# The first and the last passes of a software-pipelined graph network kernel issued from lists of their own

## The chip, the cores and the metric

The kernel runs on one core of a Trainium2 chip. The metric is the device time of one execution in microseconds (us), the median over several runs. One execution was also recorded by the hardware profiler. Engines are named as the profile names them: PE is the matrix engine, PEld its loading of weights, DVE the vector engine, ACT the engine that evaluates functions, POOL the general engine, SP the engine whose queue starts the DMAs.

## What is computed

Node features x have the shape (128 graphs, 64 nodes, 128), adjacencies adj (128, 64, 64), both float32. An adjacency has random weights between 0.05 and 5 on a symmetric, sparse pattern that includes the diagonal. Four graph layers follow one another, each behind a layer normalisation and a relu, and each is added to its input:

```python
for layer in (L0, L1, L2, L3):
    h = relu(layernorm(x))
    x = x + layer(h, adj)
# L0, continuous filters: every edge weight is expanded into 64 Gaussians, two dense
#   products with a softplus between them give a filter of 128 per edge; a node sums
#   filter * (neighbour's product), then softplus between two products
# L1, hyperbolic attention: nodes go through Moebius products and sums in the Poincare
#   ball; every edge gets a score (product, silu, product, sigmoid); a node sums its
#   neighbours' logarithmic maps by score, then silu between two products, then maps
#   back (tanh, artanh, norms and square roots per node)
# L2: product with D^-1/2 adj D^-1/2, then a dense product and a bias
# L3: messages = (adj^T xs) / degree + xr, then a dense product of [x, messages]
```

## The kernel before

**Tiling.** The 128 graphs are cut into 16 groups of 8. A group's nodes lie in tiles of 128 partitions (two graphs of 64 nodes) by 4 pairs by 128 features. The nodes of every graph are sorted by degree, so that the edges fit a fixed set of slots; layers 0 and 1 then work on slots of edges and not on all 64 by 64. A second version that works on all pairs of nodes stands behind a condition and isn't executed with this input.

**Streams and steps.** Every stage of a group is a Python generator, a stream: `load`, `order` (degrees, sorting, normalised x), `layer0`, `layer1_nodes`, `layer1_edges`, `rest1` (the end of layer 1), `rest2` (layers 2 and 3 and the store). Stages add further streams, such as `normed_x` (layer norm of the sorted x and its first product), `weights_of`, `squares`, `duo`, `filter_of` and `neighbours` in layer 0, `norm_of_h1` in `layer1_nodes`, `coefs_of`, `rows`, `scores_of` and `heads` in `layer1_edges`. The weights are prepared by four streams of their own (`slots_ranks`, `weights0`, `weights1`, `weights2`, group -1), partly through `turned_from`. A stream yields between steps; one step holds a few instructions, nearly always of one engine.

**The order.** Nothing schedules these instructions but their order in the program: the block runs under a manual schedule of PE, DVE, ACT and POOL, so each of the four works through its instructions in the order in which the steps are issued, and waits at the first one whose operand or buffer isn't ready. Only SP's DMAs are placed by the framework. The order is the long string `ORDER`, 492 entries of the form `name@offset`. `run` goes through that string once a pass, for passes -6 to 21. In pass `it` the entry `rest2@-5` issues the next step of `rest2` of group `it - 5`, if there is such a group; `weights0@=1` issues a step of a weight stream in pass 1 only. A pass therefore works on six groups at once, each in another stage. In passes -1 to 4 the later stages have no group yet, and in passes 16 and after the earlier stages have none left: the same string is issued with entries left out. A full pass issues as much as one whole group.

**Function tables.** A step can name a table of ACT ("log" for exp and ln, "silu" for silu and tanh). `step` keeps the last one named in issue order, and puts a table load (L923) in front where it changes, whichever engine the step is for.

**Lines that matter.** In `order`: the sorting product (`graphs_mm`, L1247), L1467 and L1483 (h and its copy with relu in `normed_x`), L1518 (the ranks' product) and L1530 (comparison of slots). In layer 0: the spreading of edge weights L1385, Square L1600 and Exp L1603 in `duo`, the products L1617 and L1634 with Exp L1624 and Ln between them, the multiplication L1639 and the products L1663 in `neighbours`. In layer 1: L2061 and the copies L2059 in `coefs_of`, `scores_of` L2094 to L2103, tanh L2126 in `heads`, L2197 to L2200 (two products and the Silu in `rest1`). In `rest2`: statistics L1267, L1282 (normalisation on ACT, four activations, in `normed_act`), the products of one graph each L1247 and L1254, those of a pair L1240, the scaling L1297, the store L2401. L1801 is a logarithm in `layer1_nodes`, with which a chain of some eighty short steps begins.

The two functions that decide:

```python
def step(self, name, group):
    s = self.streams[name, group]
    _, takes, _, table = s.want
    if table not in (None, self.table):
        self.table = table
        self.scalar.preload_act_table_set({...}[table])
```

Of the kernel before, what the change touches and what calls it, by code (L numbers as in the profile page):

```python
# [774 lines left out]
ORDER = """  # L775
heads20@-4 turned_from5@=2 heads20@-4 duo00@-2 rest2@-5 layer1_nodes@-3 rest2@-5 filter_of00@-2
duo02@-2 rest2@-5 product_with_bias@-3 rest2@-5 slots_ranks@=-2 coefs_of12@-4 weights_of12@-2
coefs_of12@-4 product_with_bias@-3 layer1_nodes@-3 coefs_of12@-4 weights2@=3 neighbours00@-2
rest2@-5 filter_of01@-2 turned_from0@=-4 layer1_nodes@-3 duo02@-2 filter_of00@-2 neighbours00@-2
filter_of00@-2 filter_of01@-2 slots_ranks@=0 weights0@=-2 coefs_of20@-4 layer1_nodes@-3  # L780
coefs_of20@-4 layer1_nodes@-3 layer1_edges@-4 layer1_edges@-4 layer1_nodes@-3 layer1_nodes@-3
weights1@=-5 layer1_edges@-4 layer1_nodes@-3 layer1_nodes@-3 rest1@-4 weights2@=3 layer1_nodes@-3
rest1@-4 layer1_nodes@-3 turned_from1@=-2 rest1@-4 layer1_nodes@-3 neighbours01@-2 filter_of02@-2
rest1@-4 filter_of00@-2 layer1_nodes@-3 neighbours01@-2 filter_of02@-2 filter_of01@-2 squares10@-2
layer1_nodes@-3 rest2@-5 layer1_nodes@-3 layer1_nodes@-3 turned_from2@=0 order@-1 layer1_nodes@-3
layer1_nodes@-3 layer1_nodes@-3 layer1_nodes@-3 layer1_nodes@-3 rest1@-4 layer0@-2 layer1_nodes@-3
order@-1 layer1_nodes@-3 layer1_nodes@-3 rest1@-4 layer1_nodes@-3 layer1_nodes@-3 rest2@-5
layer1_nodes@-3 layer1_nodes@-3 layer1_nodes@-3 layer1_nodes@-3 layer1_nodes@-3 layer1_nodes@-3
filter_of00@-2 layer1_nodes@-3 layer1_nodes@-3 layer1_nodes@-3 layer1_nodes@-3 layer1_nodes@-3
turned_from5@=2 layer1_nodes@-3 filter_of00@-2 layer1_nodes@-3 layer1_nodes@-3 norm_of_sum@-3  # L790
neighbours02@-2 duo20@-2 rest2@-5 weights0@=1 filter_of01@-2 rest2@-5 weights0@=1 filter_of00@-2
filter_of00@-2 filter_of01@-2 norm_of_sum@-3 rest2@-5 filter_of02@-2 neighbours02@-2 duo20@-2
layer1_nodes@-3 duo20@-2 rest2@-5 norm_of_sum@-3 layer1_nodes@-3 layer1_nodes@-3 layer1_nodes@-3
order@-1 filter_of01@-2 rest2@-5 filter_of01@-2 weights2@=2 filter_of03@-2 neighbours03@-2
weights2@=2 rest1@-4 layer1_nodes@-3 weights0@=1 filter_of03@-2 neighbours03@-2 rest1@-4
layer1_nodes@-3 filter_of03@-2 layer1_nodes@-3 squares20@-2 filter_of02@-2 order@-1 norm_of_h@-3
x_self@-4 rest2@-5 filter_of02@-2 weights0@=1 filter_of01@-2 norm_of_h@-3 filter_of02@-2
filter_of02@-2 duo22@-2 weights0@=1 layer1_nodes@-3 filter_of20@-2 duo22@-2 layer1_nodes@-3
duo22@-2 filter_of20@-2 layer1_nodes@-3 layer1_nodes@-3 order@-1 layer1_nodes@-3 filter_of02@-2
neighbours20@-2 filter_of22@-2 attention@-3 neighbours20@-2 layer1_nodes@-3 filter_of20@-2  # L800
weights2@=2 layer1_nodes@-3 order@-1 rest2@-5 layer1_nodes@-3 order@-1 layer1_nodes@-3
layer1_nodes@-3 weights0@=1 rest2@-5 attention@-3 filter_of22@-2 layer1_nodes@-3 filter_of22@-2
filter_of03@-2 turned_from1@=-4 filter_of20@-2 order@-1 duo10@-2 one_minus_z@-3 weights0@=0
one_minus_z@-3 rest2@-5 filter_of03@-2 one_minus_z@-3 layer1_nodes@-3 filter_of03@-2
filter_of03@-2 turned_from0@=-2 one_minus_z@-3 layer1_nodes@-3 order@-1 duo10@-2 one_minus_z@-3
rest2@-5 filter_of03@-2 filter_of20@-2 order@-1 filter_of20@-2 layer1_nodes@-3 layer1_nodes@-3
slots_ranks@=-5 layer1_nodes@-3 layer1_nodes@-3 layer1_nodes@-3 layer1_nodes@-3 layer1_nodes@-3
layer1_nodes@-3 layer1_nodes@-3 layer1_nodes@-3 layer1_nodes@-3 layer1_nodes@-3 order@-1
attention@-3 neighbours22@-2 turned_from3@=-2 order@-1 duo10@-2 rest2@-5 attention@-3
neighbours22@-2 order@-1 duo12@-2 weights2@=2 turned_from4@=1 filter_of10@-2 rest2@-5  # L810
filter_of11@-2 duo12@-2 filter_of10@-2 rest2@-5 filter_of10@-2 order@-1 filter_of11@-2
neighbours10@-2 filter_of22@-2 weights0@=-2 rest2@-5 layer1_nodes@-3 rest2@-5 neighbours10@-2
filter_of10@-2 rest2@-5 order@-1 filter_of22@-2 layer1_nodes@-3 filter_of22@-2 filter_of10@-2
duo12@-2 layer1_nodes@-3 rest2@-5 filter_of11@-2 rest2@-5 filter_of12@-2 neighbours11@-2 order@-1
filter_of11@-2 layer1_nodes@-3 layer1_nodes@-3 turned_from3@=-2 layer1_nodes@-3 weights1@=0
filter_of12@-2 neighbours11@-2 filter_of12@-2 squares12@-2 filter_of10@-2 rest2@-5 weights2@=2
filter_of10@-2 layer1_nodes@-3 filter_of10@-2 layer1_edges@-3 coefs_of02@-3 order@-1
filter_of11@-2 order@-1 rest2@-5 filter_of11@-2 coefs_of00@-3 order@-1 rest1@-4 rest2@-5
filter_of13@-2 neighbours12@-2 neighbours13@-2 filter_of13@-2 neighbours12@-2 filter_of13@-2
neighbours13@-2 filter_of12@-2 rows00@-3 filter_of13@-2 turned_from4@=1 order@-1 rest2@-5  # L820
filter_of11@-2 filter_of12@-2 layer0@-2 rows00@-3 filter_of11@-2 filter_of12@-2 filter_of13@-2
# [49 lines left out]
class Weave:  # L871
# [63 lines left out]
    def run(self, order, groups):  # L935

        steps = [step.rsplit("@", 1) for step in order.split()]
        for it in range(-6, groups + 6):
            for name, off in steps:
                if off[0] == "=":  # L940
                    if int(off[1:]) == it:
                        self.step(name, -1)
# [1511 lines left out]
```

## Time and profile before

| What | Value |
|---|---|
| Time, median of 3 runs | 1788.97 us (1787.3, 1788.97, 1789.33) |
| Time of the profiled execution | 1789.83 us |
| Its span (first to last instruction) | 1788.0 us |
| PE busy | 1580.1 us (88%), 10231 matmuls |
| DVE busy | 1576.3 us (88%), 4872 instructions |
| ACT busy | 1496.0 us (84%), of it 92 table loads of 1283 ns |
| POOL busy | 413.3 us (23%) |
| Mean granted clock of PE | 0.935 of full speed |
| Chain that ended last | PE 48%, ACT 30%, DVE 14% |

All times of instructions, stretches and waits are from the profiled execution, counted from the start of its span. Its time is 1.83 us above its span, and 0.86 above the median. The page gives busy times over the whole span, in 40 slices of 44.7 us, the chain of work that ended last, and the costliest lines; the trace gives a row for each run of equal instructions (start, duration, engine, line, operation, output and inputs, and behind it in brackets how long the engine had been idle and which instruction ended that).

### The profile page before, as it was taken

The page shows a single profiled execution, that of the slowest core. Times are in us where ns is not written, and L with a number is a line of the kernel's source. Part 1 is how long each engine was busy: PE and PEld are TensorE (multiplying, and loading weights), DVE is VectorE, ACT ScalarE, POOL GpSimd, SP SyncE. Part 2 cuts the span into 40 slices and gives each one's busy share as a digit, 9 for nine tenths or more (in the row PEclk, how much of TensorE's full clock was granted, in tenths as well). Part 3 has the DMA queues.
Part 4 walks back from the last instruction along what each step waited for, and adds up shares of the span by engine and source line. Part 5 has one row for each costly group of instructions (what it writes and reads, how often), then busy time and mean ns, then how long its engine had stood idle before and what let it go on. Part 6 is the DMA issues. An engine that isn't in the chain of part 4 may idle for free.

```text
span 1788.0 us, 30233 instructions
## 1 busy us (share of the span) xinstructions
PE 1580.1 (88%) x10231; PEld 855.9 (48%) x10231; DVE 1576.3 (88%) x4872; ACT 1496.0 (84%) x2784; POOL 413.3 (23%) x717
## 2 busy tenths in 40 slices
PE   3969888998989899898989899898989989896853
PEld 2424444545545455454545454554545455454542
DVE  5659799999999999999999999999999999988853
ACT  2858898989899898989899898989989898986632
POOL 1010113123221413223121312322141322302221
PEclk8979999999999999999999999999999999997865
DMA  2000202011110202011020201111020201102110
GB/s 62 6 1 7 57 7 54 11 43 24 27 46 16 58 7 57 17 34 34 16 58 10 60 10 38 30 27 46 16 58 1 50 18 29 36 7 58 33 37 9
DMA packets 57173, 54.22 MB, mean 30 GB/s; under 512 B 13616, under 2 KB 40624, under 8 KB 57008
## 3 DMA queue, kind: packets, MB, share of 16 engines
q1 hardware_dynamic: 57008, 52.19, 11.8%
q8 instruction: 83, 1.36, 0.3%
q14 instruction: 82, 0.67, 0.1%
HBM read 7.61 MB, written 4.19 MB: 7 GB/s over the span
## 4 chain that ended last, share of the span: by engine, by line
PE 48%; ACT 30%; DVE 14%; issue 3%; POOL 2%; DMA 2%; SPq 1%; DVEq 0%; ACTq 0%; POOLq 0%
PE big L1634 7%; PE sm L1240 7%; PE big L2094 6%; PE big L2076 5%; PE big L1617 5%; PE big L1663 4%; ACT ex L1624 4%; PE sm L2120 3%; ACT ex L1627 3%; PE big L2098 3%; ACT e L1600 3%; DVE ex L1639 2%; ACT ra L1669 2%; ACT e L1603 2%; PE sm L1247 2%
## 5 line engine op out<-in xcount | busy, mean ns | idle before, releaser
L1634 PE MATMUL big<-ex,w2T 128*128 128x512 f32 (+1 forms) x768 | 296.5, 519 | 10.4 <-DVE den L1707 5.6
L1639 DVE SCALAR_TENSOR_TENSOR ex<-big,c_L_gnn_b,ra 128x1024 f32<-128x1024 f32 (+1 forms) x160 | 198.4, 1240 | 28.4 <-PE big L1634 27.0
L1617 PE MATMUL big<-e,w1T 64*128 64x512 f32 (+1 forms) x768 | 187.2, 581 | 10.9 <-ACT e L1603 8.3
L1634 PEld LDWEIGHTS big<-ex,w2T 128*128 128x128 f32 x768 | 134.2, 190 | 122.2 <-issue 72.5
L1624 ACT ACTIVATE ex<-big,c_L_gnn_b 128x1024 f32<-128x1024 f32 (+1 forms) x160 | 174.5, 1091 | 7.4 <-PE big L1617 6.9
L2094 PE MATMUL big<-va,U 64*128 64x512 f32 (+1 forms) x768 | 175.3, 532 | 4.9 <-DVE va L2079 4.9
L1663 PE MATMUL big<-va,a 64*128 64x512 f32 (+1 forms) x768 | 176.8, 560 | 2.9 <-ACT va L1584 1.8
L2103 ACT ACTIVATE ex<-big,c_L_gnn_att_b 128x1024 f32<-128x1024 f32 (+1 forms) x160 | 167.6, 1078 | 9.8 <-PE big L2098 9.4
L2098 PE MATMUL big<-slot_r,Sx 64*128 64x512 f32 (+1 forms) x768 | 165.9, 507 | 0.0
L1627 ACT ACTIVATE ex<-ex 128x1024 f32<-128x1024 f32 (+1 forms) x160 | 165.4, 1033 | 0.1
L1669 ACT ACTIVATE ra<-big 128x1024 f32<-128x1024 f32 (+1 forms) x160 | 160.2, 1001 | 3.5 <-PE big L1663 1.7
L1398 DVE TENSOR_TENSOR ex<-ex 128x512 f32<-128x512 f32 (+1 forms) x256 | 140.4, 554 | 1.4
L2214 POOL TENSOR_TENSOR w<-w,hh 128x512 f32<-128x512 f32 x16 | 22.1, 1379 | 454.7 <-DVE w L2206 441.6
L923 ACT ACT_TABLE_LOAD x92 | 118.0, 1283 | 2.2 <-PEq L2442 0.7
L2059 DVE COPY_PREDICATED att<-oh,th 128x256 f32<-128x256 uint16 x256 | 111.4, 446 | 8.2 <-DMA th<-row 8.0
L2076 PE MATMUL big<-oh,pqs 64*64 64x512 bf16 (+1 forms) x1152 | 115.0, 337 | 0.0
L1663 PEld LDWEIGHTS big<-va,a 64*128 64x128 f32 x768 | 73.2, 198 | 87.1 <-issue 47.1
L2079 DVE COPY_PREDICATED va<-slot_r,big 128x1024 f32<-128x1024 uint32 (+1 forms) x96 | 105.2, 1097 | 5.7 <-PE big L2076 5.5
L2120 PE MATMUL sm<-ex,aw2b 128*32 128x512 f32 (+1 forms) x640 | 98.0, 593 | 11.0 <-ACT ex L2103 11.0
L2098 PEld LDWEIGHTS big<-slot_r,Sx 64*128 64x128 f32 x768 | 73.6, 187 | 59.9 <-issue 59.9
L1254 PE MATMUL big<-adjT,v 64*128 64x64 f32 x256 | 31.5, 424 | 74.5 <-ACT v L1282 74.5
L1617 PEld LDWEIGHTS big<-e,w1T 64*128 64x128 f32 x768 | 65.4, 197 | 63.9 <-issue 28.6
(570 smaller groups left out, 3678.0 us busy)
## 6 DMA issues: line engine op xcount, KB each, us to landing
th<-row SPq DMA_DIRECT2D x128, 256.0 KB, 3.5
th<-row SPq DMA_DIRECT2D x64, 104.0 KB, 2.2
x<-in_x_dram SPq DMA_DIRECT2D x16, 256.0 KB, 2.8
out_dram<-v SPq DMA_DIRECT2D x16, 256.0 KB, 2.3
adj<-in_adj_dram SPq DMA_DIRECT2D x16, 128.0 KB, 2.4
e<-in_L_gnn_att_w_dram SPq DMA_DIRECT2D x2, 64.0 KB, 4.4
bR<-in_L_gnn_mlp_w_dram SPq DMA_DIRECT2D x2, 64.0 KB, 3.6
wupd<-in_L_gnn_W_upd_dram SPq DMA_DIRECT2D x1, 128.0 KB, 3.4
```

Of the source, the lines that this page charges most:

```text
L1617: T.matmul(dst, lhsT=w1T[HALF[h], :], rhs=e[HALF[h], b, 0:W], start=True, stop=True)
L1624: act(ex[:, :, 0:wide], pre[:, :, 0:wide], AF.Exp, bias=b1)
L1627: act(ex[:, :, 0:wide], ex[:, :, 0:wide], AF.Ln, bias=1.0)
L1634: T.matmul(wf[:, b, cols], lhsT=w2T, rhs=ex[:, b if c < 2 else b ^ j, cols], start=True, stop=True)
L1639: V.scalar_tensor_tensor(two.rearrange("q (j r) -> q j r", j=2), wf[:, :, 0:wide], b2s, ra[:, :, 0:wide], ALU.add, ALU.mult)
L1663: T.matmul(nb[:, b, at * W:at * W + W], lhsT=rf[rows, p + j, :], rhs=factors[0][rows, k + j, :], start=True, stop=True)
L1669: act(ra[:, :, 0:wide], nb[:, :, 0:wide], AF.Copy)
L2076: T.matmul(rk[h, k, 0:W], lhsT=pqs[h, s, p, :], rhs=oh[h, p, at:at + W], start=s == 0, stop=s == 2)
L2094: T.matmul(pre[:, b, col], lhsT=U[h, p + k, :], rhs=coefs[h, k, :], start=True, stop=False)
L2098: T.matmul(pre[:, b, col], lhsT=Sx[s][h, p + k, :], rhs=slot_r[h, at:at + W], start=False, stop=s == 1)
L2103: act(a[:, :, 0:wide], pre[:, :, 0:wide], AF.Silu, bias=ab1)
L2120: T.matmul(sl[here, 0:wide], lhsT=aw2b, rhs=a[:, b, 0:wide], start=True, stop=True)
```

## The change

The string `ORDER` loses its entries for one pass only and is used for passes 6 to 13 alone. All that the passes before it issued now stands in a list `HEAD`, and all that the passes behind it issued in a list `TAIL`. The lists are written out: each entry gives a stream by its number in `NAMES` and a group (in `HEAD` as it is, in `TAIL` counted from 16), and is one step. `HEAD` has 1476 steps and `TAIL` 2159 of the 7228 in all. They hold the same steps as before, in another order.

```diff
 ORDER = """
-heads20@-4 turned_from5@=2 heads20@-4 duo00@-2 rest2@-5 layer1_nodes@-3 rest2@-5 filter_of00@-2
...
+heads20@-4 heads20@-4 duo00@-2 rest2@-5 layer1_nodes@-3 rest2@-5 filter_of00@-2 duo02@-2 rest2@-5
...
 """
+CYCLES = range(6, 14)
+NAMES = """
+heads20 turned_from5 duo00 rest2 layer1_nodes filter_of00 duo02 product_with_bias slots_ranks
...
+"""
+HEAD = """
+8@-1 8@-1 8@-1 18@-1 18@-1 18@-1 43@-1 43@-1 20@-1 24@-1 24@-1 20@-1 15@-1 15@-1 15@-1 79@0 15@-1
...
+"""
+TAIL = """
...
+3@-1 3@-1
+"""
...
-    def run(self, order, groups):
-
-        steps = [step.rsplit("@", 1) for step in order.split()]
-        for it in range(-6, groups + 6):
+    def run(self, groups):
+
+        names = NAMES.split()
+        steps = [step.rsplit("@", 1) for step in ORDER.split()]
+
+        def listed(order, base):
+            for step in order.split():
+                k, g = step.split("@")
+                self.step(names[int(k)], base + int(g))
+
+        listed(HEAD, 0)
+        for it in CYCLES:
             for name, off in steps:
-                if off[0] == "=":
-                    if int(off[1:]) == it:
-                        self.step(name, -1)
-                elif 0 <= it + int(off) < groups:
-                    self.step(name, it + int(off))
+                self.step(name, it + int(off))
+        listed(TAIL, groups)
...
-        w.run(ORDER, GROUPS)
+        w.run(GROUPS)
```

Two short stretches show how the lists differ, written as stream@group#step:engine. The first steps of `normed_x` of group 0, before and after:

```text
before  order@0#16 to #18:DVE  turned_from4  order@0#19:DVE  normed_x@0#0:DVE
        sums_of_columns@0#0:POOL  normed_x@0#1 to #3:POOL  normed_x@0#4:PE  normed_x@0#5:ACT
after   order@0#13:ACT  sums_of_columns@0#0:POOL  normed_x@0#0:DVE  normed_x@0#1 to #3:POOL
        normed_x@0#4:PE  normed_x@0#5:ACT  order@0#14:DVE  order@0#15:PE  order@0#16 to #18:DVE
```

And in pass 18, where only the last groups are left:

```text
before  rest1@14#8:PE  ...  scores_of00@15#0:PE  scores_of01@15#0:PE  ...
        scores_of00@15#1:ACT  scores_of01@15#1:ACT
after   rest1@14#8:PE  ...  scores_of00@15#0:PE  scores_of00@15#1:ACT
        scores_of01@15#0:PE  scores_of01@15#1:ACT
```

## The prediction

> **What bounds the kernel now.** I read the slices of the page first. The kernel is full in the middle and thin at both ends:
>
> ```profile
> PE   3969888998989899898989899898989989896853
> ...
> DVE  5659799999999999999999999999999999988853
> ...
> PEclk8979999999999999999999999999999999997865
> ```
>
> One slice is 44.7 us. The first four slices and the last four are the only ones with low digits. Then I took the busy times by stretch. Passes were found by counting each engine's instructions in the order of the list: pass 6 begins at 411 us, pass 14 at 1230. Each full pass takes 102.3 us: the stores of groups 0 and 11 begin at 371.2 and 1496.7, and (1496.7 - 371.2) / 11 = 102.3. Columns are the stretch, its length, then busy us of PE, PEld, DVE, ACT, POOL, then the granted clock.
>
> ```profile
> 0.00:45.00 45.00, 17.77 (x98) 10.66 (x100) 26.14 (x88) 13.39 (x21) 8.78 (x34) 0.85 0.26 62
> 45.00:70.00 25.00, 24.86 (x155) 12.52 (x153) 14.36 (x28) 22.32 (x28) 0.19 (x1) 0.93 0.04 11
> 70.00:125.00 55.00, 38.46 (x151) 18.31 (x146) 30.60 (x79) 31.38 (x58) 6.27 (x7) 0.78 0.00 1
> ...
> 411.00:1230.00 819.00, 770.41 (x5108) 416.37 (x5104) 776.28 (x2401) 747.33 (x1396) 206.61 (x347) 0.97 0.13 32
> 1230.00:1536.00 306.00, 287.80 (x1910) 155.86 (x1914) 291.54 (x902) 279.35 (x519) 76.04 (x128) 0.97 0.12 30
> ...
> 1635.00:1707.00 72.00, 51.70 (x355) 31.56 (x355) 58.65 (x224) 40.71 (x97) 18.31 (x35) 0.77 0.16 40
> 1707.00:1740.00 33.00, 20.09 (x115) 15.37 (x115) 14.80 (x46) 9.81 (x27) 8.19 (x10) 0.63 0.09 21
> ```
>
> In the middle DVE is busy 776 of 819 us and PE 770: both bound, and that part is untouched. Outside it PE is busy about 344 us in the first 411 and 465 in the last 558; at the middle's 94% these would take 366 and 494 us. So about 45 us at the front and 64 at the back are lost to chains with nothing beside them. That is the ceiling for any new order, not the forecast.
>
> **What the change moves.** The two lists hold exactly the steps that the first six and last seven passes issued, with the same places where they begin and end, so all arithmetic and the 818 us between stay. The queue of DMA issues on SP keeps its order. No group is started a pass earlier: the work of the same engine that stands ahead of a step differs by 0.4 to 1.6 us on average in every pass. So only waits between neighbours can change. The program has 86 table loads where it had 92; the six that go are three silu/log pairs of the last passes. I walked the places where an engine sits idle, with the durations of the trace.
>
> **A, fill, -1.9 us.** The rows that matter, from the timeline (start, duration, engine, line):
>
> ```profile
> 31.65 1.08 POOL L1467 TENSOR_TENSOR a<-xp,o_mv 128x512 f32<-128x512 f32 x1
> ...
> 34.29 3.50 DVE L1385 TENSOR_TENSOR va<-oh,adjT 128x1024 f32<-128x1024 bf16 x3
> ...
> 36.75 1.14 ACT L1483 ACTIVATE a<-sm,sr 128x128 f32<-128x128 f32 x4 [2.22 <-PE sm L1240]
> ...
> 40.80 1.28 ACT L923 ACT_TABLE_LOAD   x1
> ...
> 42.10 1.06 ACT L1603 ACTIVATE e<-e 128x1024 f32<-128x1024 f32 x1
> ```
>
> HEAD puts normed_x of group 0 directly behind the copy of xp (ACT, ends 23.0) instead of behind the slot comparisons (L1530); weights1's last DVE step also goes ahead. Its DVE part (1.2) then ends at 24.2, not 30.2; POOL's h comes 2.5 us later at 26.7, the transposes (1.1) end at 27.9. But L1518 now stands behind them on PE: it ends at 28.2 instead of 25.9, and the DVE work after it (0.42 + 2.36 + 0.27 + 3.00) ends at 34.3, where it ended before. So the spread L1385 gains nothing; the stall moved from PE to DVE. What gains is ACT: L1483 is done at 32 instead of 37.9, so squares00 runs at 35.5, squares02 behind its operand at 36.7, the first Square of duo at 37.8, the load at 38.9, the Exp at 40.2, against 42.10. That is 1.9. From 45 to 70 PE is busy 24.86 of 25 us, so all that follows moves along and nothing is added. Bounds: 3.6 gained (the PE wait before L1617 at 43.2), 1.0 lost if DVE waits longer for L1518.
>
> **C, first nodes chain, -1.3.** Between 106 and 120 us ACT waits four times for the chain of layer1_nodes. The Exp of group 1's first duo (L1603, 1.04 us) runs at 120.47, behind that chain; HEAD issues it at about 112.5, in a gap. ACT is busy 24.8 of the 25 us from 125, so the microsecond counts; 0.3 more comes from the DVE step L1304, no longer behind a weights2 step. Bounds 0 and -1.8.
>
> **B and D, 45-92 and 125-411: 0.** PE or ACT is full and the work is the same. Bounds +3 and -3: small reorderings in passes 3 to 5.
>
> **E, passes 14 to 17, -2.** Each pair of loads removed looks like this:
>
> ```profile
> 1286.67 2.57 ACT L923 ACT_TABLE_LOAD   x2
> ...
> 1289.26 1.11 ACT L1624 ACTIVATE ex<-big,c_L_gnn_b 128x1024 f32<-128x1024 f32 x1
> ```
>
> Six loads of 1.28 us are 7.7 us of ACT. ACT is busy 279 of 306 us there, DVE 292 and PE 288: not ACT's time but DVE's sets the pass, so I take a quarter of it. To save the pair, the list puts rest1's product (L2197) 7 us of PE work later in two of the three cases; its Silu (L2200) stands where it stood on ACT. Bounds: -7.7 if ACT's time is all on the path, +8 by the second rival.
>
> The Trainium skill, "ScalarE: Activation LUTs", "What ACT_TABLE_LOAD costs", gives 1283 ns for a load and 1380 ns more for a drain, 2.66 us in all; by it E's ceiling would be 16 us as an estimate. The rows agree on the first and show no second: L1624 begins 20 ns after the loads.
>
> **F, last group's nodes, -1.7.** On ACT at 1630 us, and on the same chain five microseconds later:
>
> ```profile
> 1635.07 0.59 ACT L2126 ACTIVATE row<-sm,hab 128x416 f32<-128x416 f32 x1
> ...
> 1636.20 1.65 ACT L1282 ACTIVATE v<-x,k_s,k_r 128x128 f32<-128x128 f32 x4 [0.54 <-DVE k_s L2309]
> ...
> 1637.87 1.28 ACT L923 ACT_TABLE_LOAD   x1
> ...
> 1639.16 0.21 ACT L1801 ACTIVATE nn<-nn 128x8 f32<-128x8 f32 x1
> ```
>
> TAIL moves norm_of_h1 (1.28 us of ACT) into the 1.10 us wait before L2272 at 1629.8, which brings the heads at 1635.07 to about 1634.3 (-0.8). It then puts the load and L1801 ahead of rest2's L1282. The logs follow at 1636.1 instead of 1639.2, but L1282 still stands before the next ACT step of the chain (at_p, 1640.2), which ends up at 1638.5. Of the 1.7, 0.8 is the first move and 0.9 the second. DVE is dense for the ten microseconds after it, then the chain runs alone to 1672, so I let the 1.7 through. Bounds 0 and -2.9. What is late next is PE: from 1672.7 to 1701.8 it has no gap, so TAIL's other moves there (rows00 earlier, last copies) are worth 0.
>
> **G, last two groups side by side, -2.1.**
>
> ```profile
> 1710.92 1.66 DVE L2061 SCALAR_TENSOR_TENSOR th<-th,oh 128x832 f32<-128x832 f32 x1 [1.91 <-DMA th<-row]
> 1715.74 1.12 DVE L1297 SCALAR_TENSOR_TENSOR v<-sm,dn,x 128x128 f32<-128x128 f32 x4
> ```
>
> L1297 (rest2 of group 14) is ready at 1713.0, when PE's L1240 ends, and waits behind seven DVE instructions of group 15. TAIL puts it directly behind L2061: 1713.1. The permutation steps follow (0.42, PE 0.37, DVE 0.45 + 0.48), L1247 starts at 1715.7 instead of 1719.2. The steps of group 15 that it overtook then take DVE until 1718.9, so the statistics L1267 start there, not at 1721.8, and L1282 at 1721.7 instead of 1724.7. On PE the transposes stand behind rest1's L1254, which ends at 1723.1, and end at 1724.7 against 1726.8: 2.1 remain, and carry through L1240 and L2383 to rest1's L2197 (1732.5 before). After L2197 the chain of group 15 is alone and its order is the same: 0 to the end. Bounds 0 and -3.5.
>
> **The sum:** -1.9 - 1.3 + 0 - 2 - 1.7 - 2.1 = -9.0 us. It is made on the profiled execution, 1789.83 us with a span of 1788.0, which is 0.86 above the median. Taken off the median of 1788.97: 1780.0.
>
> The Trainium skill, "TensorE: Matmul & The Clock Gate", Part 1, says that a window of about 3.4 us without PE work halves its clock. This trace agrees in kind: the clock is 0.63 in 1707-1740, and eight matmuls of L1240 take 2.08 us at 1710.9 but 1.16 at 1735.5. By the rule denser ends would also run faster, perhaps 3 us more as an estimate; the sum has none of it.
>
> **Rivals.** *Hidden anyway:* each walk assumes that the chain it shortens is the one that sets the end. If only G survives, the gain is 2.1 us: 1787. For it speaks A, where one moved wait came straight back. What a measurement can tell from no change is about 0.2%, 3.6 us. Chance 0.15.
>
> *Tighter passes (slower):* passes 4, 5 and 14 to 17 ran at the middle's 102.3 us, and the lists re-interleave them too. In the one list a consumer stands behind enough other work; some now stand closer. In pass 14 the DVE mask L1515 of order stands seven steps further up, about 1.7 us of DVE work sooner against the ACT copy it reads; DVE is in order, so all behind it waits, and DVE has only 4.8 us of slack a pass (14.5 idle in three). One or two such waits a pass, 2.5 us, in six passes are +15; with E gone and A, C, F, G kept (-7.0) that is +8: 1797. It decides above 1.8 us a pass. Against it: I found only two to five such places a pass, none above 2.6 us. Chance 0.21.
>
> *Looser passes:* the same re-interleaving takes a third of DVE's 4.8 idle us from six passes, -10 more: 1770. Chance 0.20.
>
> That the change does nothing is excluded by the order of the two programs: some steps move on every engine but SP.
>
> **The numbers.** The forecast, -3.6 to about -14, has 0.44; with the looser passes faster is 0.64, same 0.15, slower 0.21. All bounds at once would reach 1767 and 1801; they will not meet. The range is 1768 to 1796: about 0.07 below it, 0.13 above. The likeliest case alone is 1775 to 1785.
>
> **What would show it.** Right: Exp L1603 first at about 40 us; stores of rest2 still 102.3 apart in the middle; L2197 of the last group still about 50 us before the last store is issued (1732.5 and 1782.5 now), with L1247 of group 14 some 4.8 us behind the start of L2061 instead of 8.3; 86 loads. Wrong: the first L1603 not earlier; the stretch from pass 14 to the store of group 12 longer than before; new DVE waits on ACT copies (L1515) or on PE (L1639) in passes 4, 5, 14 to 17.

## The result and the profile after

| Kernel | Median, us | Runs, us |
|---|---|---|
| before | 1788.39 | six, 1787.3 to 1789.33 |
| after | 1797.28 | six, 1795.17 to 1798.64 |

The ratio is 1.0048, with an interval of 1.0037 to 1.0058: slower by 8.9 us, where 1780.0 was forecast. The profiled execution took 1797.08 us, its span 1795.3. Lines of the kernel after have numbers 217 higher (L1603 is L1820, L1639 is L1856); the experiments' kernels have shifts of their own.

From the page of the kernel after, the busy times, the slices and the chain that ended last:

```profile
PE 1585.7 (88%) x10231; PEld 848.8 (47%) x10231; DVE 1596.2 (89%) x4872; ACT 1493.9 (83%) x2778; POOL 419.8 (23%) x717
...
PE   5879898998989899998989899898989989897863
...
DVE  5759799999999999999999999999999999998863
...
PE 40%; ACT 29%; DVE 22%; issue 3%; POOL 2%; DMA 2%; SPq 1%; DVEq 0%; ACTq 0%
```

The first two slices and those at the end are fuller, as the prediction wanted. But DVE is busy 19.9 us longer than before (1576.3) with the same 4872 instructions, and its share of the chain went from 14% to 22%.

I took the end of every step in both traces and compared them pass by pass. A minus says that the kernel after was ahead: -6.4 us at 117 to 122 us, -5.2 in pass 2, -2.1 in pass 4, +2.0 in pass 6, +0.4 in passes 10 to 13, +6.4 in pass 15, +11.6 in pass 17, +6.4 in pass 19, +7.2 at the end. So the fill gained more than forecast and lost it all by pass 6; passes 14 to 17 lost 11; the end gave back 5.

The windows of three passes of the old tail, one line a pass (stretch, length, then busy us of PE, PEld, DVE, ACT and POOL, the clock, the DMA share, GB/s), before:

```profile
1245.00:1347.00 102.00, 96.15 (x639) 51.97 (x638) 97.09 (x302) 93.29 (x175) 25.63 (x43) 0.97 0.13 32
1347.00:1449.20 102.20, 96.43 (x639) 52.20 (x638) 97.07 (x302) 93.37 (x175) 25.57 (x43) 0.97 0.12 30
1449.20:1551.40 102.20, 96.44 (x639) 52.34 (x638) 96.51 (x298) 93.25 (x175) 25.56 (x43) 0.97 0.11 28
```

and between the same steps after:

```profile
1244.80:1353.40 108.60, 99.93 (x647) 52.28 (x646) 102.13 (x311) 94.56 (x175) 27.56 (x43) 0.97 0.12 30
1353.40:1458.50 105.10, 95.60 (x642) 50.27 (x645) 100.26 (x299) 94.11 (x175) 27.97 (x43) 0.98 0.12 29
1458.50:1562.70 104.20, 97.04 (x637) 51.02 (x637) 99.43 (x298) 90.04 (x172) 26.46 (x43) 0.97 0.11 28
```

The passes are 11.5 us longer, DVE is busy 11.1 us longer in them, and its idle time hardly changes (15.7 and 16.1 us). PE and ACT have nearly the same work (by the counts in the rows PE 9 matmuls more, ACT 3 instructions fewer) and more idle time. Whatever happened, happened inside what the page calls DVE's busy time.

**Theory 1, pairs.** The timeline of DVE shows how. Three steps of `rest1` of group 11 (L2261, L1327, L1329) with what stands between them, before:

```profile
1414.22 0.16 DVE L2261 TENSOR_SCALAR d_s<-d_hn 128x4 f32<-128x4 f32 x1
1414.29 0.44 DVE L2059 COPY_PREDICATED att<-oh,th 128x256 f32<-128x256 uint16 x1
1414.63 0.16 DVE L1327 TENSOR_SCALAR ah<-d_s 128x4 f32<-128x4 f32 x1
1414.70 0.42 DVE L1740 TENSOR_SCALAR a<-a 128x512 f32<-128x512 f32 x1
1415.03 0.17 DVE L1329 RECIPROCAL ah<-ah 128x4 f32<-128x4 f32 x1
```

and the same steps after:

```profile
1421.94 0.16 DVE L2478 TENSOR_SCALAR d_s<-d_hn 128x4 f32<-128x4 f32 x1
1422.01 0.42 DVE L1957 TENSOR_SCALAR a<-a 128x512 f32<-128x512 f32 x1
1422.34 0.16 DVE L1544 TENSOR_SCALAR ah<-d_s 128x4 f32<-128x4 f32 x1
1422.54 0.18 DVE L1546 RECIPROCAL ah<-ah 128x4 f32<-128x4 f32 x1
```

An instruction's record is its entry in the trace, from its start to its end. An instruction whose operand is older begins some 80 ns before its predecessor's record ends: L1957 at 1422.01, L2478 ends at 1422.10. L1546 reads what L1544, directly ahead of it, wrote. It begins 40 ns after that record's end. Over the whole trace of before the first kind has a median of -83 ns, the second of +34 ns: 117 ns a pair, two neighbours of which the second needs the first. A step that overwrites what the one ahead has read or written begins as late, and counts too. In the old string steps of other streams stand between such neighbours, and TAIL and HEAD put many side by side. By the programs there are 785 such pairs before and 975 after, 66 more in HEAD and 124 more in TAIL. The lost overlap counts as busy time, which is why DVE looks busier with the same work.

The rivals that the experiments had to exclude: the waits on PE and ACT that the prediction's slower rival named (theory 2), the table loads, and the changed order as such, whatever its pairs (theory 3). The clock is none: the mean granted clock is 0.941 in the profiled execution, and was 0.935 before.

The account of DVE's time between two marks (the same step of `layer1_nodes` in two groups) is read from the traces. The columns add up to the length: the records' durations; the gaps inside pairs, with the pairs' number; the other gaps up to 60 ns, nearly all overlaps; and the waits over 60 ns.

| Stretch | Kernel | Length, us | Records | Pairs | Other gaps | Waits |
|---|---|---|---|---|---|---|
| three passes, HEAD | before | 296.5 | 326.5 | +5.1 (129) | -53.1 | 18.0 |
| | after | 304.9 | 326.0 | +7.8 (188) | -47.7 | 18.7 |
| three passes, TAIL | before | 306.4 | 354.1 | +5.4 (130) | -63.1 | 10.1 |
| | after | 317.9 | 358.0 | +8.3 (213) | -55.9 | 7.5 |

In HEAD's stretch 59 more pairs cost 2.7 in their own gaps and 5.4 in overlap that is gone, 8.1 of 8.4 us. The waits are a net sum there. DVE waits 2.82 us for PE at 124 us, where it did not wait before, and the other waits of the stretch got shorter by 2.1. That wait alone takes the lead at the start of the stretch from 6.4 to 3.6 us; e1 has it too, with 1.69 us, and e3, which leaves HEAD's order at 117 us, has none. So for HEAD no run separates the wait's share from that of the pairs. In TAIL's stretch 83 more cost 2.9 and 7.2, 10.1 of 11.5; the waits are 2.6 less, and the records 3.9 more, of which seven instructions that now fall between the marks are 2.3, and steps held by POOL (last section) 2.2, less small differences.

### The profile page after: what moved, and what is told of

Its sections match the earlier page's. It is cut to its first block, busy times and chain, and to the rows that moved or that the text cites. A ratio compares the mean times of both kernels' runs of the same rounds, so it can differ in the third digit from the quotient of the medians.

```text
span 1795.3 us, 30197 instructions
## 1 busy us (share of the span) xinstructions
PE 1585.7 (88%) x10231; PEld 848.8 (47%) x10231; DVE 1596.2 (89%) x4872; ACT 1493.9 (83%) x2778; POOL 419.8 (23%) x717
## 4 chain that ended last, share of the span: by engine, by line
PE 40%; ACT 29%; DVE 22%; issue 3%; POOL 2%; DMA 2%; SPq 1%; DVEq 0%; ACTq 0%
PE big L1851 7%; PE sm L1457 6%; PE big L2311 5%; PE big L2293 4%; PE big L1834 4%; DVE ex L1856 3%; PE big L1880 3%; ACT ex L1841 3%; PE sm L2337 3%; ACT ex L1844 2%; ACT e L1817 2%; PE big L2315 2%; ACT ra L1886 2%; ACT ex L2320 2%; DVE ex L1615 2%
## 5 line engine op out<-in xcount | busy, mean ns | idle before, releaser
L1851 PE MATMUL big<-ex,w2T 128*128 128x512 f32 (+1 forms) x768 | 301.8, 524 | 7.6 <-DVE den L1924 3.8
L1856 DVE SCALAR_TENSOR_TENSOR ex<-big,c_L_gnn_b,ra 128x1024 f32<-128x1024 f32 (+1 forms) x160 | 198.0, 1238 | 26.6 <-PE big L1851 24.1
L2320 ACT ACTIVATE ex<-big,c_L_gnn_att_b 128x1024 f32<-128x1024 f32 (+1 forms) x160 | 167.8, 1078 | 21.1 <-PE big L2315 20.7
```

Of the source, the lines that this page charges most:

```text
L1851: T.matmul(wf[:, b, cols], lhsT=w2T, rhs=ex[:, b if c < 2 else b ^ j, cols], start=True, stop=True)
L1856: V.scalar_tensor_tensor(two.rearrange("q (j r) -> q j r", j=2), wf[:, :, 0:wide], b2s, ra[:, :, 0:wide], ALU.add, ALU.mult)
L2320: act(a[:, :, 0:wide], pre[:, :, 0:wide], AF.Silu, bias=ab1)
```

## The experiments

Ratios are to the kernel before, run on the same chip, with 95% intervals.

| Kernel | Pairs | Median, us | Before, us | Ratio |
|---|---|---|---|---|
| e1_head | 851 | 1790.68 | 1789.23 | 1.0010 (1.0000 to 1.0019) |
| e2_tail | 909 | 1796.29 | 1789.23 | 1.0038 (1.0023 to 1.0054) |
| e3_ends | 803 | 1781.05 | 1789.23 | 0.9957 (0.9944 to 0.9971) |
| e4_apart | 835 | 1805.69 | 1789.23 | 1.0094 (1.0079 to 1.0110) |
| e5_adjacent | 937 | 1810.89 | 1789.07 | 1.0115 (1.0099 to 1.0132) |
| e6_loads | 785 | 1789.44 | 1789.07 | 0.9999 (0.9990 to 1.0008) |
| e7_last_first | 800 | 1777.82 | 1789.07 | 0.9933 (0.9919 to 0.9946) |
| e8_tail_adjacent | 913 | 1809.24 | 1790.29 | 1.0108 (1.0093 to 1.0124) |
| e9_from_pass17 | 805 | 1776.96 | 1790.29 | 0.9925 (0.9912 to 0.9939) |
| e10_last_first_again | 800 | 1777.31 | 1790.29 | 0.9930 (0.9917 to 0.9944) |
| e11_fill_pairs | 481 | 1789.02 | 1788.92 | 0.9999 (0.9990 to 1.0008) |
| e12_fill_else | 785 | 1793.94 | 1788.92 | 1.0030 (1.0019 to 1.0040) |
| e13_free_before | 729 | 1786.51 | 1788.64 | 0.9983 (0.9974 to 0.9992) |
| e14_free_adjacent | 809 | 1793.39 | 1788.64 | 1.0027 (1.0016 to 1.0039) |
| e15_free_after | 883 | 1795.02 | 1788.64 | 1.0029 (1.0017 to 1.0041) |

e13 has 56 pairs fewer than before, not the 53 of its expectation.

### One list at a time: e1_head, e2_tail

In the kernel after, the other list's steps are put back in the order of the old string (the lists shortened to a description here):

```diff
 HEAD = ...                      # e1_head keeps it
-TAIL = ...
+TAIL = """the same steps in the order of the old string"""
# e2_tail: the same with HEAD
```

> HEAD as in the changed kernel, and behind pass 13 the one list as before. Theory 1 (pairs): a DVE step that stands directly behind the DVE step whose result it reads starts 34 ns after that one's end in both traces, any other 83 ns before its predecessor's end, so each such pair costs 117 ns of DVE; the program of before has 785 pairs, this one 851, and 66 x 0.117 = 7.7 us are lost in passes 3 to 5, against the 6.4 us that the fill gains up to 122 us. Theory 2 (waits): the loss in passes 3 to 5 is stalls behind other engines, such as 2.8 us of DVE before the filter's multiplication at 124 us. Both expect the shift that the changed kernel shows in its middle: +0.4 us against before, within 1 us. If the two lists act on one another, it is off by more than 2 us.

> The one list as before up to pass 13, and TAIL behind it. From the shift of the changed kernel's steps: +11 us in passes 14 to 17, -4.5 in the last two passes, in all +6.7 us against before. Theory 1 explains the +11 by 24 + 33 + 26 + 29 = 112 more pairs in these four passes, 112 x 0.117 = 13.1 us, less what the idle time of DVE takes; theory 2 by waits for PE and ACT, of which the trace of the changed kernel shows no more on DVE in passes 14 to 17 than before (about 14 against 18 us). Time: +5 to +8 us by both.

With HEAD alone the steps are ahead by 5.0 us in pass 2, behind by 2.7 in pass 6, and 1.5 behind from there to the end. With TAIL alone the steps stay within 1.5 us of before up to pass 13, then they are at +1.5, +4.9, +8.2, +9.6 in passes 14 to 17, and +6.4 at the end. The two add up to the change (1.5 and 7.1 us by the medians, 8.9 in all). Each list gains at its outer end and loses where it re-interleaves passes that were already full.

### The ends only: e3_ends

HEAD is kept for its first 275 steps, up to 117 us, and TAIL for its last 396 (passes 18 to 20); all between goes back to the old order (described, not printed, here too).

```diff
-HEAD = <1476 steps of the new list>
+HEAD = <first 275 of the new list, the rest in the old order>
-TAIL = <2159 steps of the new list>
+TAIL = <old order, then the last 396 of the new list>
```

> HEAD's order only up to step 20 of layer1_nodes of group 0 (117 us), then the one list's order for what is left of passes 1 to 5; the one list for 6 to 17; then TAIL's order for the steps that passes 18 to 20 issued. 803 pairs against 785 and 975. If passes 3 to 5 and 14 to 17 are where the lists lose and nothing else, both ends keep their gain: -6.4 at the front, -4.5 at the end, +2 for 18 pairs: -9 us, between -11 and -6. If a lead at the front is taken back by the full passes whatever their order (the changed kernel's shift went from +2.0 in pass 6 to +0.4 in pass 9, so a pass has some play), only the end is left: -5 to -3.

1781.05: 8.2 us faster than before, and 16 faster than after. The lead of 7.3 us that the fill makes now survives through all passes to pass 17, and the last passes add 3 (the profiled execution, 1779.39, is the fastest of the five). So the gains forecast for the two ends are there, and they carry. What ate them was the middle of each list.

### Pulling the pairs apart again: e4_apart

Both new lists, with a rule that takes a DVE step of another stream from up to five places further on where a stream's next DVE step would follow directly:

```diff
+def other(self, todo):
+    dve = [key in self.streams and self.streams[key].want[0] == DVE for key in todo[:6]]
+    if dve[0] and todo[0] == self.last:
+        for j in range(1, len(dve)):
+            if (dve[j] and todo[j] not in todo[:j] and self.ready(self.streams[todo[j]])):
+                return j
+    return 0
...
-            for step in order.split():
-                k, g = step.split("@")
-                self.step(names[int(k)], base + int(g))
...
+            while todo:
+                self.step(*todo.pop(self.other(todo)))
```

> Both lists of the changed kernel, with one rule in their issue: where the next step is a DVE step of the stream that issued the last DVE step, the next ready DVE step of another stream among the five entries behind it is issued first. 835 pairs against the changed kernel's 975; PE, ACT and POOL keep their order, and the table loads stay at 86. Theory 1: 140 pairs x 0.117 = 16.4 us less of DVE, three quarters of it on the path: -12 us against the changed kernel, -8 to -16, so -3 against before. Theory 2: the held back steps only come later, and nothing that DVE waits for is earlier: 0 to +4 against the changed kernel, +9 to +13 against before.

It has 140 pairs fewer than the kernel after and is 8.4 us slower: theory 1's number was missed, with the wrong sign, and theory 2's 0 to +4 as well. The account of TAIL's three passes shows what the rule gives and takes there:

| Kernel | Length, us | Records | Pairs | Other gaps | Waits |
|---|---|---|---|---|---|
| after | 317.9 | 358.0 | +8.3 (213) | -55.9 | 7.5 |
| e4_apart | 317.9 | 356.5 | +5.9 (152) | -59.5 | 15.1 |

61 pairs fewer give back 2.4 and 3.6, 6.0 us, as the theory has it. The waits grow by 7.6, so this stretch is as long as in the kernel after. The loss comes elsewhere: HEAD's stretch is 2.3 us longer, with some 5 us more of waits, and the middle keeps e4 3.6 us behind the kernel after; of the 5 us that the last passes gave the kernel after, e4 gets 2. In the answer on DVE's waits in that stretch (us in total, times, longest), three of after:

```profile
DVE e L2236 <- ACT pqs L2234: 2.1, 2, 1.5
...
DVE ex L1856 <- PE big L1851: 0.4, 2, 0.2
DVE rt L2207 <- ACT e L2195: 0.3, 1, 0.3
```

and the same of e4_apart:

```profile
DVE e L2244 <- ACT pqs L2242: 3.1, 2, 2.1
DVE ex L1864 <- PE big L1859: 2.2, 4, 0.9
...
DVE rt L2215 <- ACT e L2203: 1.4, 1, 1.4
```

A step pulled ahead had its place in the list, but not yet its operand, as far as these rows tell; they are 3.9 of the 7.6 us. Parting a pair with a step that isn't ready did not pay here.

### More pairs, nothing else moved far: e5_adjacent, e8_tail_adjacent

The opposite experiment on the kernel before. If the stream that ran last on DVE has its next DVE step one or two places further on, that step is issued first. In e5 this holds in passes 6 to 13, for `rest1` and `rest2`; in e8 in passes 14 to 17, for `filter_of` too.

```diff
+def same(self, todo):
+    for j in range(1, min(3, len(todo))):
+        if (todo[j] == self.last and self.last[0] in ("rest1","rest2") and todo[j] in self.streams
+                    and self.streams[todo[j]].want[0] == DVE and self.ready(self.streams[todo[j]])
+                    and todo[j] not in todo[:j]):
+            return j
+    return 0
```

> The program of before with one rule in passes 6 to 13 alone, where the changed kernel has the same list as before: a DVE step of rest1 or rest2 whose stream issued the last DVE step is moved up by one or two entries, directly behind it. 937 pairs against 785, 19 more in each of the eight passes; PE, ACT and POOL keep their order, and every moved step comes earlier, the step it passes later by 0.1 to 0.2 us. Theory 1 (a pair costs 117 ns of DVE): 152 x 0.117 = +17.8 us, or less by what the 5 us of idle DVE in a pass take up: +10 to +18. Theory 2 (only waits for other engines cost): nothing that waits for PE, ACT or POOL moves by more than 0.2 us: 0, within 2 us.

> The program of before with the rule of the run in the middle passes, now in passes 14 to 17 alone, where TAIL lost 10 to 11 us, and for the streams of rest1, rest2 and filter_of: a DVE step is moved up by one or two entries, directly behind the DVE step of its own stream. 128 pairs more than before (913 against 785); TAIL as it is has 124 more, 112 of them in these passes. All else is the old order, table loads included. Theory 1: at 117 ns a pair +15 us, at the 136 ns of the run in the middle +17: +10 to +18. Theory 2 (TAIL loses by waits for other engines that its order makes): these waits are not made here: 0 to +4.

Both are some 20 us slower. e5's steps fall behind evenly over passes 6 to 14, up to 20.7 us, and stay there; with 152 pairs more that is 136 ns each. In e8 passes 14 to 17 take 20.1 us more; with 128 pairs more that is 157 ns each. The chains that ended last on the pages of e5 and e8:

```profile
DVE 36%; PE 28%; ACT 27%; issue 4%; POOL 2%; DMA 1%; SPq 0%; DVEq 0%; ACTq 0%; POOLq 0%
```

```profile
PE 41%; DVE 26%; ACT 25%; issue 3%; POOL 2%; DMA 2%; SPq 1%; DVEq 0%; ACTq 0%; POOLq 0%
```

DVE led 14% of it before. More than 117 ns a pair comes out because waits join in:

| Stretch | Kernel | Length, us | Records | Pairs | Other gaps | Waits |
|---|---|---|---|---|---|---|
| seven middle passes | before | 717.3 | 825.7 | +12.4 (301) | -145.4 | 24.5 |
| | e5_adjacent | 736.0 | 826.4 | +16.9 (431) | -137.6 | 30.3 |
| three passes, TAIL | e8_tail_adjacent | 323.4 | 357.2 | +8.7 (226) | -56.5 | 14.1 |

In e5 130 more pairs are 12.3 of 18.7 us, new waits 5.8. In e8 96 more are 9.9 of 17.0 against before, waits 4.0, records 3.1. e8 has 13 pairs more than the kernel after in these passes and takes 5.5 us more; its waits are 14.1 us and not 7.5. So TAIL's order, apart from its pairs, waits less.

### Are the table loads worth anything? e6_loads

The kernel before, but `rest1`'s first product no longer names a table, so 28 of 92 loads go, 35.9 us of ACT:

```diff
-        yield on(PE, "sm", table="silu")
+        yield on(PE, "sm")
```

> The program of before, in which the product L2197 of rest1 no longer names the silu table (its Silu still does): 64 table loads against 92, and no pair of loads in a row; nothing else moves. This is the prediction's part E by itself, on 28 loads and not 6: 28 x 1.283 = 35.9 us less of ACT. As the prediction took it, a quarter on the path: -9 us. If ACT's time is on the path: -20 and more. If DVE and PE set the pass and ACT's time is free: 0 to -2.

ACT is busy 1460.8 us where it was 1496.0, and the time is the same. From the page of e6:

```profile
PE 1582.9 (89%) x10231; PEld 857.4 (48%) x10231; DVE 1575.8 (88%) x4872; ACT 1460.8 (82%) x2756; POOL 413.5 (23%) x717
```

The 28 loads cost nothing on the path. So six fewer, as in TAIL, should be worth 0.

### The best order found: e7, e9 and e10

e7 and e10 are one kernel: e3_ends with the steps of group 15's `rest1` ahead of those of group 14's `rest2` where both stand ready in the last passes. e9 keeps TAIL's order already from `norm_of_h1` of group 15 on, in pass 17. The first place where e7's TAIL departs from that of e3, with the numbers of the list written as stream and group:

```diff
...
-rest2@14 rest2@14 coefs_of12@15 rest2@14 layer1_edges@15 rest2@14 coefs_of20@15 layer1_edges@15
-layer1_edges@15 rest2@14 rest1@15 rest1@15
+coefs_of12@15 layer1_edges@15 coefs_of20@15 layer1_edges@15 layer1_edges@15 rest1@15 rest1@15
...
```

> The kernel with the ends alone (HEAD to 117 us, TAIL's order from pass 18), in which from step 8 of rest2 of group 14 on the steps of group 15 are issued as if 8 us earlier and those of rest2 of group 14 as if 4 us later. In the run with the ends alone, rest1 of group 15 had its two products L2197 ready at 1716.6 us and they began at 1722.0, behind rest2 of group 14 on PE; before that its last scores waited for 2.9 us behind two steps of rest2 of group 14 on DVE. If the chain of the last group sets the end, both waits go: -8 us against the kernel with the ends alone, -16 against before (-12 to -18). If the chain of group 14 is late next, or PE at a lower clock takes it back: -8 to -10 against before.

> The kernel with the last group first, with TAIL's order taken over 20 us earlier, from norm_of_h1 of group 15 on (1630 us in the trace of before), which is the prediction's part F: norm_of_h1 in the wait before L2272, and the logarithms of group 15 ahead of rest2's L1282. The prediction's value for it: -1.7 us against the kernel with the last group first; in the changed kernel the chain of layer1_nodes of group 15 was 3.4 us earlier behind these steps than ahead of them, and lost it again within 20 us. If the nodes' chain is followed by a dense stretch of PE whatever its start: 0.

> The kernel with the last group first once more, on the same chip as the run before, for the comparison of the two: -11 us against before, within 1.5 us.

e7 gains 3 us on e3 and e10 repeats it (1777.82 and 1777.31), less than expected: `rest1`'s product of group 15 begins 4 us earlier, at 1718.2, but it stays only 1.5 ahead afterwards. e9 and e10 differ by 0.35 us, which is not measurable, so moving `norm_of_h1` (term F) is worth nothing. These kernels are 11 to 13 us (0.7%) below the kernel before and 20 below the kernel after. The slices of e9:

```profile
PE   5869898998989899898989999898989989897863
...
DVE  5759799999999999999999999999999999988863
```

The ends are as full as those of the kernel after, and DVE is busy 1579.9 us, not 1596.2.

### Is a pair's hole really empty? e11_fill_pairs, e12_fill_else

The kernel before, with 38 tiny copies a pass in passes 6 to 13, 304 in all, which nothing reads. In e11 they stand between the two steps of pairs, in e12 at as many other places on DVE.

```diff
+def fill():
+    k = next(scraps) % 64
+    V.tensor_copy(scrap[:, k:k + 1], series_b)
```

> The program of before, and in passes 6 to 13 one more tiny DVE instruction (a copy of one column of 128 partitions into scrap that nobody reads) in each of 38 places a pass, 304 in all: between a DVE step and the dependent DVE step directly behind it. In the traces a small independent instruction takes about 80 ns of DVE, start to start. Theory 1: between the two steps of a pair DVE stands still from 83 ns ahead of the end of the first to 34 ns behind it; the copy fits into these 117 ns and costs nothing: 0 to +3 us. If a pair leaves no hole, the copies cost as much here as anywhere.

> The same 304 copies, but each between two DVE steps of which the second doesn't read the first, 38 a pass, spread over the passes. Theory 1, with DVE's time on the path of a full pass: 304 x 0.08 = +24 us, at least +12 if half of it goes into idle time. If DVE's time isn't on the path: 0, and then the hole of a pair would cost nothing either.

In the timeline of e11, one of them:

```profile
804.97 0.15 DVE L1593 SCALAR_TENSOR_TENSOR ah<-ah,ah 128x4 f32<-128x4 f32 x1
805.04 0.14 DVE L1195 COPY scrap<-series_b 128x1 f32<-128x1 f32 x1
805.15 0.16 DVE L1595 TENSOR_TENSOR ah<-ah,ah 128x4 f32<-128x4 f32 x1
```

L1595 begins 0.18 us after L1593, with a copy between them; L1546 above began 0.20 after L1544 with nothing between. 304 instructions more cost nothing (1789.02 and 1788.92), though DVE's busy time grows by 10.2 us, 34 ns each: the hole is real and can be filled. At other places they cost 5.0 us, 16 ns each. That is less than the 12 to 24 expected. In seven middle passes DVE's waits over 60 ns are some 11 us shorter in e12 than before, so most of the copies fell into waits.

### Dependence or order? e13, e14, e15

In all three, 21 DVE steps of `rest1` read only finished tiles and write five scratch tiles in turn; so part of layer 1 is not computed. The number, size and order of instructions stay as they are. e13 has the order of before, e14 that of e5, e15 that of after.

```diff
-V.reciprocal(E, E)
+V.reciprocal(next(own), s)
...
-V.scalar_tensor_tensor(num, E, 1.0, s, ALU.add, ALU.mult)
+V.scalar_tensor_tensor(next(own), s, 1.0, s, ALU.add, ALU.mult)
```

> The order of before. Left out: the 21 steps of artanh_over in rest1 no longer use each other's results; each reads s or hn and writes one of five tiles in turn, with the same kind and size of instruction, so layer 1 isn't computed. 53 pairs of dependent neighbours fewer in the whole program (732 against 785), nothing else moves. Theory 1 (the dependence costs): -2 to -7 us against before. Theory 3 (the order costs): 0.

> The order of the run in which steps of rest1 and rest2 were moved up in passes 6 to 13 (+20 us there), with the same part left out as in the run before: 80 pairs more than that one, where the run with whole artanh_over had 152 more than before. Theory 1: 80 x 0.136 = +11 us against the order of before with the same part left out. Theory 3 (the moved order costs): +20 as it was.

> The changed kernel, with the same part left out: 154 pairs more than the order of before with the same part left out, where the whole kernels differ by 190; in passes 14 to 17 it is 86 and not 111. Theory 1: the changed kernel's +8.9 us falls by 36 x 0.117 = 4 us, to about +5 (+3 to +7). Theory 3: +9 as it was.

e13 gains 2 us, nearly all of it in the last passes. e14 is 6.9 us above e13, where the same two orders with their dependences stood 21.8 apart: with 72 of the 152 pairs undone, two thirds of e5's loss are gone, and the order is the same to the step. So that part of the loss comes from the dependence. The 80 pairs left cost 86 ns each (in the seven middle passes the account finds 2.7 of 7.2 us in pairs and 4.5 in longer records, which I can't explain; by the length, the 67 more pairs of these passes cost 107 ns each). e15 is 8.5 us above e13. Theory 1 expected 3 to 7; theory 3's 9 is nearer. The account of TAIL's stretch:

| Kernel | Length, us | Records | Pairs | Other gaps | Waits |
|---|---|---|---|---|---|
| e13_free_before | 305.4 | 353.4 | +5.2 (124) | -62.6 | 9.4 |
| e15_free_after | 316.3 | 358.3 | +7.3 (186) | -58.5 | 9.2 |

62 more pairs make 6.2 us, 100 ns each. The rest is 4.9 us in the records, half of it the seven instructions that moved into the stretch. Only 27 pairs of TAIL's three passes were undone by this edit, and the waits took 1.7 of the 3.6 us that those gave back (against after). So in TAIL about 10 of 11.5 us sit in pairs by the account, but no experiment took all of them away alone. How much would come back if one could stays open: that the pairs cost time is shown by e5 and e14, that they are what TAIL lost is read from the account.

## Why the prediction was wrong

**The step that failed** is "B and D, 45-92 and 125-411: 0" together with the middle of E. The prediction held that "only waits between neighbours can change", and that moved steps cost nothing where an engine is full, since "the work is the same". The work is the same and the time isn't: how the same DVE instructions follow one another sets how far they overlap. B and D measured +8.4 us in three passes, outside their bounds of 3. E measured +11.5 where -2 stood, outside its upper bound of +8; the -2 itself, for six loads, did not come either, as 28 loads were worth 0 in e6. I had read the instructions' durations and the waits between engines, and not the distance from one start to the next.

**A** (-1.9) had the right mechanism and was too small: the first Exp moved by 4.55 us, more than the bound of 3.6. In the timeline of after:

```profile
31.79 2.36 DVE L1602 TENSOR_TENSOR va<-oh,adjT 128x1024 f32<-128x1024 bf16 x2
...
36.26 1.28 ACT L1135 ACT_TABLE_LOAD   x1
37.55 1.06 ACT L1820 ACTIVATE e<-e 128x1024 f32<-128x1024 f32 x1
```

The walk let the spread (L1385, now L1602) start at 34.3 as before. It started at 31.79. The same five slot comparisons ran ahead of it in both kernels. Before, they took 0.27 and then 3.00 us, with two instructions of POOL beside them (the first is L1467 of the prediction's rows):

```profile
31.34 3.00 DVE L1534 TENSOR_TENSOR oh<-pos,slot_k 128x324 bf16<-128x324 bf16 x4
32.81 1.27 POOL L1469 TENSOR_TENSOR xp<-xp,r_L_gnn_bd 128x512 f32<-128x512 f32 x1
```

After, POOL was done at 27.5 us, and the five took 1.52:

```profile
30.31 1.52 DVE L1751 TENSOR_TENSOR oh<-pos,slot_k 128x120 bf16<-128x120 bf16 x5
```

Two of the four took 1.09 and 1.38 us beside POOL and take 0.37 and 0.31 here. The 3.00 that the sum carried over was not their own time; the last section has more of this.

**C** (-1.3) was right in kind: the Exp of group 1 runs at 106.56, ahead of the chain. The 6.4 us of lead at 117 to 122 us leave 1.9 for it beside A's 4.55, by subtraction, just over its bound of 1.8. The lead then shrank at once; in the timeline of DVE in pass 3 of the kernel after, behind 2.82 us of waiting for PE:

```profile
127.00 1.28 DVE L1856 SCALAR_TENSOR_TENSOR ex<-big,c_L_gnn_b,ra 128x1024 f32<-128x1024 f32 x1 [2.82 <-PE big L1851]
```

The same instruction before waited for nothing:

```profile
130.59 1.28 DVE L1639 SCALAR_TENSOR_TENSOR ex<-big,c_L_gnn_b,ra 128x1024 f32<-128x1024 f32 x1
```

**F** (-1.7): the chain was 3.4 us less late at the logs and had lost that twenty us later. e9 against e10 shows nothing. **G** (-2.1): the mechanism was right in each row, and L1464 begins 4.9 us behind L2278, where 4.8 was forecast. The last passes gave 4.5 us, more than its bound of 3.5; in e3, without the lost middle, 3.

```profile
1721.70 1.75 DVE L2278 SCALAR_TENSOR_TENSOR th<-th,oh 128x832 f32<-128x832 f32 x1 [3.15 <-DMA th<-row]
1723.98 1.27 DVE L1514 SCALAR_TENSOR_TENSOR v<-sm,dn,x 128x128 f32<-128x128 f32 x4 [0.53 <-PE sm L1457]
```

The sum as measured, on the spans: -6.4 from A and C, +8.4 in HEAD's passes 3 to 5, -2 regained in the middle, +11.5 in TAIL's passes, -5 at the end, +0.8 in the last chain alone; +7.3 us. Where the middle of both lists is put back (e3), the ends bring 8.2 us by the median. The forecast for the ends alone was A, C, F and G, 7.0. That these are close is partly luck: A was too small by 2.65 us and F was worth nothing.

**The slower rival** had the place (passes 4, 5 and 14 to 17), the price (2.5 us a pass forecast, 2.8 measured in HEAD's three passes and 3.8 in TAIL's) and the time (1797). It had the mechanism only in one place, the wait for PE in pass 3 above; in sum its waits did not grow, and so the match of the time is luck. From the groups by line, its first witness, the mask of `order` (idle before it in us, and what ended that), before:

```profile
L1515 DVE TENSOR_SCALAR o<-adjT 128x256 bf16<-128x256 f32 x16 | 4.7, 293 | 29.0 <-ACT adjT L1207 29.0
```

and after:

```profile
L1732 DVE TENSOR_SCALAR o<-adjT 128x256 bf16<-128x256 f32 x16 | 4.7, 291 | 14.6 <-ACT adjT L1424 14.6
```

It waits half as long, and L1639's wait on PE fell from 27.0 to 24.1 us. "Some now stand closer" was true of DVE's own steps among themselves, which I had not looked at. What would have told it stood in the rows all along: the start of an instruction against the end of the one before, where no wait stands in brackets.

**A rule that would have misled further.** By the medians above, an instruction that needs its predecessor's result begins 34 ns behind that record's end, and another 83 ns ahead of it. The Trainium skill, "VectorE: DVE Perf Modes", section "The DRAIN you can't avoid", says that a semaphore after each instruction costs nothing (eight copies take 13.88 us with one after each and with one after the last alone), and the page's "Rules for kernel authors" say to minimize the number of DVE instructions, not the semaphores. By that, TAIL and HEAD would cost nothing. In this case the number of instructions doesn't decide: 304 more cost nothing in e11 and 5.0 us in e12, and 152 more dependent neighbours cost 21.8 us in e5 with the same number.

## What to carry to other kernels

In a kernel with an in-order vector engine that is nearly full, don't put two short dependent steps of a chain side by side: a small independent instruction between them was free in e11, and a pair cost 0.09 to 0.16 us here, with the waits that follow. Judge a new order by the distance from start to start of its rows and not by busy time, which counts a lost overlap as work. Reorder the thin ends, where a chain runs alone, and leave the full passes as they are, which is what paid here (e3, e7); where pairs must be parted, use only steps whose operands are there.

## What else the chip showed

- The gap between dependent neighbours is not DVE's alone. On ACT it is +32 ns where others begin 95 to 118 ns ahead of the end, on POOL +78 against about -45 (medians).
- Some short DVE steps that meet a POOL instruction are held until it ends. In the timeline of after, POOL's row, then two of DVE's:

```profile
1306.17 1.49 POOL L1684 TENSOR_TENSOR a<-xp,o_mv 128x512 f32<-128x512 f32 x1
1306.68 1.00 DVE L2451 TENSOR_TENSOR k__14054<-k__14054,ur 128x4 f32<-128x4 f32 x1
...
1307.71 0.16 DVE L2454 TENSOR_TENSOR d_xy<-uh,k__14054 128x4 f32<-128x4 f32 x1
```

  L2451 lasts 1.00 us, not 0.16, and ends with L1684. The Trainium skill, "SBUF — State Buffer", section "SBUF: two separate sides", describes such a lock on a shared port between the two engines. It has a small part in the change. In the fill the slot comparisons of term A that took 3.00 us before stood beside two such instructions. In TAIL's three passes seven steps were over 0.2 us longer before than after, 5.1 us in all, and eight longer after than before, 7.3, each beside POOL where it was long: 2.2 of the 11.5 us.
- Spans of kernels with the same fill differ by up to 2.7 us in their first passes, from one execution to another, and keep that difference to the end. One profiled execution doesn't settle a microsecond.
